# Seven block products for eight at two more sites of a four-layer graph network, and adjacency loads issued from another queue

## The chip, the core and the metric

The kernel runs on one NeuronCore of a Trainium2 chip. The metric is the device time of one execution in microseconds (us); lower is better. The engines are named as the profile names them: PE is TensorE (its matmuls; PEld is its weight loads), DVE is VectorE, ACT is ScalarE, POOL is GpSimd, SP is SyncE. ACTq and SPq are the queues of ScalarE and SyncE when they issue DMAs (transfers between the chip's main memory and its on-chip memory).

## What is computed

Thirty-two independent graphs ("batches" b = 0 to 31) of 512 nodes with 128 features pass through four layers. `x` holds the features and `adj` a dense 512 x 512 matrix for each graph. Everything is fp32. Each layer adds its result to its input:

```
h = relu(layernorm(x));  x = x + leaky_relu(normalised(adj + I) @ (h @ W) + b)             # layer 0
h = relu(layernorm(x));  x = x + tanh([adj @ in(h), node(h), adj^T @ out(h)] @ W_upd + b)   # layer 1
h = relu(layernorm(x));  x = x + f4                                                        # layer 2
h = relu(layernorm(x));  x = x + GRU(m, h), m = tanh(adj @ (h @ W_msg + b))                # layer 3
```

Layer 2 is itself a stack of four inner layers. With f0 = h, each computes f_new = tanh(A1 @ (f @ ws) + f @ wn + A2 @ (f @ wd) + b), where A1 and A2 are `adj` scaled to unit rows and to unit columns. The third inner layer takes [f2, f1] as its input and the fourth [f3, f1, f0], so their projections have 2 x 128 and 3 x 128 input features. The GRU of layer 3 has gates r and z, each a sum of a product of h and a product of m, and a third term whose two products stay apart.

## The kernel before, in words

**Planning.** The function `program(b)` (L389) doesn't issue instructions. It records operations with `op()`: an engine, an assumed duration, the buffers read and written, and a function that issues the instruction. For all 32 batches these go into one list. `Plan.order()` then plays the list through a model of the engines: each engine takes, from the operations whose inputs are ready and whose buffers have a free place, the one with the lowest key. The key is a due time (one batch every `PERIOD`, less the length of the work still behind the operation); the first batch's loads carry a `rank` that puts them ahead of everything. What comes out is one fixed order per engine. On the chip each engine works through its own order and never past an instruction that is still waiting. `places` says how many buffers of each kind exist ("bank": 8 PSUM banks of 512 fp32 per partition, "s2": 32 tiles of 128 x 512, "s4": 6 tiles of twice, "s8": 10 tiles of four times that size); `kept` says how many of a kind a younger batch has to leave free for each batch that is older and unfinished.

**A batch's work.** Loads of `x` (256 KB), `adj` as tile `a` and its transpose as tile `aT` (1 MB each, in two pieces of 512 KB; four of 256 KB for batch 0) go through `load()` at L405 and L413, all on SP. `adjt` is loaded a second time as `aT2` for layer 3, since layer 2 scales `a` and `aT` in place. `degree` (L608) and the squared norms (L687) are ACT passes over `a` and `aT`, called `sq`. A layernorm (L417 to L451) is DVE statistics, a power on POOL, and four ACT pieces `h` (L448). `aggregate` (L492) is four PE products of 512 columns into one PSUM bank. `turned` (L453) transposes through a DVE instruction and two DMA steps by way of main memory; in the first three and last two batches PE transposes instead (L484).

**Projections.** `paired_rows` (L510) makes both projections (ws and wd side by side, 256 columns wide) of the nodes, four chunks of 128 nodes each. For the third inner layer that is 4 chunks x 2 inputs = 8 products of 256 columns, with two DVE additions of bias (L523). The gates (L793 to L802) are, in all batches, 4 chunks of four products: two of 256 columns for r and z, and two of 128.

**`seven`** (L528) replaces a block product [x1 x2] @ [[b11, b12], [b21, b22]] of 2 x 2 blocks, each half of x being 256 nodes: seven block products stand in for eight, with sums of weights prepared once (`t_sb`, filled by `setup`, L375 to L387) and sums of inputs and of products made on DVE while it runs. A block product is two PE instructions of 128 columns (L567), so a use of `seven` has 14 of them, in four PSUM banks, and 14 DVE instructions: two of 512 columns (L580, L593) and twelve of 256 columns (L545). It needs five more s2 tiles. Before the change only the site "last" uses it: f1 and f0 of the fourth inner layer, as soon as f1 is known (L741). `program` already holds the code for the sites "mid" (L721) and "gates" (L781); both ask whether their name is in `SEVEN`.

Of the kernel before, what the change touches and what calls it, by code (L numbers as in the profile page):

```python
# [19 lines left out]
B, N, D = 32, 512, 128  # L20
NC = N // P
# [5 lines left out]
SMALL = 16  # L27


SEVEN = {"last": 0 * 5 * D}  # L30

T_COLS = 5 * D * len(SEVEN)

# [6 lines left out]
W_L2 = []  # L40
# [51 lines left out]
class Plan:  # L92
# [28 lines left out]
    def bank(self, name):  # L121
        return self.buf("bank", name=f"ps_{name}")

    def op(self, engine, us, emit, reads=(), writes=(), kb=0.0, rank=None, later=0.0):

        o = Op()
        o.engine, o.us, o.land, o.emit, o.batch, o.rank, o.later = engine, us, 0.0, emit, self.batch, rank, later
        if kb:  # L130
            o.us, o.land = max(us, kb / self.RATE), self.TRANSFER
        o.after, o.next, o.bufs = {}, [], []
        for group, written in ((reads, False), (writes, True)):
            for item in group:
                buf, part = item if isinstance(item, tuple) else (item, None)
                if written and buf.old is not None:
                    for other, _, _ in buf.old.uses:
                        o.after[other] = True
                for other, p, w in buf.uses:
                    if (w or written) and other is not o and (part is None or p is None or part & p):  # L140
                        o.after[other] = True
                buf.uses.append((o, part, written))
                if buf not in o.bufs:
                    o.bufs.append(buf)
        self.ops.append(o)
        return o
# [82 lines left out]
def gnn_stack(  # L229
# [11 lines left out]
    nc = tc.nc  # L241
    const = ctx.enter_context(tc.tile_pool(name="const", bufs=1))
    sb = ctx.enter_context(tc.tile_pool(name="sb", bufs=1))
    psum = ctx.enter_context(tc.tile_pool(name="psum", bufs=1, space=bass.MemoryType.PSUM))
    dram = ctx.enter_context(tc.tile_pool(name="dram", bufs=1, space=bass.MemoryType.DRAM))
    plan = Plan(sb, psum, {"bank": 8, "s2": 32, "s4": 6, "s8": 10}, {"bank": 1, "s2": 5, "s4": 0, "s8": 0})

    w_sb = const.tile([P, W_COLS], F32, name="w_sb")
    c_sb = const.tile([P, C_COLS], F32, name="c_sb")
# [1 line left out]
    rf_sb = const.tile([P, len(L2_CHUNKS) * 2 * D], F32, name="rf_sb")  # L251
# [15 lines left out]
    def t_tt(n, pointers=0):  # L267
        return 0.065 + 0.058 * pointers + n / 960
# [13 lines left out]
    def op(*args, **kwargs):  # L282
        return plan.op(*args, **kwargs)

    def const_buf(name, ap):
        b = Buf(plan, name, name, None)
        b.tile, b.slot = ap, 0
        return b

    W1, W2F, W3, CS, RS, RF, CF, TS, ID, NH = (const_buf(n, t) for n, t in (  # L290
        ("w1", w_sb), ("w2", w_sb), ("w3", w_sb), ("c_sb", c_sb), ("r_sb", r_sb), ("rf_sb", rf_sb),
        ("cf_sb", cf_sb), ("t_sb", t_sb), ("ident", ident), ("neg_half", neg_half)))

    def mm(ps, out_of, lhs, rhs, n, start, stop, reads, later=0.0):
        op("PE", t_mm(n), lambda: nc.tensor.matmul(out_of(ps.ap()), lhs(), rhs(), start=start, stop=stop),  # L295
           reads, [ps], later=later)

    def blocks(site):


        if site == "gates":
            return [c + k * D for c in (W_L3_HH, W_L3_IH) for k in range(2)], W3, (r_sb, R_L3_G), (RS, {2})
        i, k = {"mid": (2, 0), "last": (3, 1)}[site]
        at = W_L2[i][0] + k * 2 * D
        return [at + k * D for k in range(4)], W2F, (rf_sb, i * 2 * D), RF

    def setup():


        op("POOL", 1.0, lambda: make_identity(nc, ident), [], [ID])  # L310
        op("POOL", 0.2, lambda: nc.gpsimd.memset(neg_half, -0.5), [], [NH])
        first = W_L2[0][0]

# [29 lines left out]
        for i, (k, (proj, upd)) in enumerate(zip(L2_CHUNKS, RAW_L2, strict=True)):  # L343
# [23 lines left out]
            else:  # L367
# [5 lines left out]
                rf_sb[:, i * 2 * D:(i + 1) * 2 * D], ps.ap()[:, :2 * D]), [ps], [RF])  # L373
        for site, at in SEVEN.items():
            (b11, b12, b21, b22), wbuf, (bias, c), bbuf = blocks(site)  # L375
# [13 lines left out]
    def program(b):  # L389
        plan.batch = b  # L390

        def buf(tag, shape=(P, N), name=None):
            return plan.buf(tag, shape, name)
# [9 lines left out]
        pieces = NC if b == 0 else 2  # L403

        def load(dst, src, kb, rank):  # L405

            n = NC // pieces
            for k in range(pieces):
                s = slice(k * n, (k + 1) * n)
                op("SP", 0.4, lambda s=s: nc.sync.dma_start(dst.ap()[:, s, :], src[:, s, :]),  # L410
                   [], [(dst, set(range(NC)[s]))], kb=kb / pieces, rank=None if b else rank)

        op("SP", 0.4, lambda: nc.sync.dma_start(xt.ap(), x[b]), [], [xt], kb=256, rank=None if b else 0)  # L413
        load(a, adj[b], 1024, 1)
        load(aT, adjt[b], 1024, 4)

        def moments(xin, v8):  # L417
# [35 lines left out]
        def turned(m, name):  # L453


            blk, mT = buf("s2", rows_shape, "blk"), buf("s2", rows_shape, name)
            op("DVE", t_tt(N), lambda: nc.vector.transpose(
                blk.ap().rearrange("p b (c r) -> p c b r", c=NC), m.ap().rearrange(
                    "p c (b s) -> p c b s", b=NC) if len(m.shape) == 3 else m.ap().rearrange("p (c b s) -> p c b s", c=NC, b=NC)),
               [m], [blk])  # L460
            bounce = buf(f"turn_{name}", rows_shape)

            def away(k):
                if bounce.tile is None:
                    bounce.tile = dram.tile([P, NC, P], F32, name=bounce.name, tag=f"{bounce.kind}_{bounce.slot}", bufs=1)
                nc.sync.dma_start(bounce.tile[:, k, :].rearrange("(b s) n -> s b n", b=NC), blk.ap()[k * P // NC:(k + 1) * P // NC])

            for k in range(NC):
                op("SP", 0.4, lambda k=k: away(k), [blk], [(bounce, {k})], kb=64)
            op("SP", 0.4, lambda: nc.sync.dma_start(mT.ap(), bounce.tile), [bounce], [mT], kb=256)  # L470
            return mT

        def turned_cols(mT):
# [36 lines left out]
        def paired_rows(nodes, wcols, wbuf, bias, bbuf, col, sd=None):  # L510


            held, sd = sd, sd or buf("s4", (P, NC, 2 * D), "sd")
            for h in range(NC // 2):
                ps = plan.bank("sd")
                for j in range(2):
                    c = 2 * h + j
                    for k, nk in enumerate(nodes):
                        mm(ps, lambda t, j=j: t[:, j * 2 * D:(j + 1) * 2 * D],
                           lambda nk=nk, c=c: nk.ap()[:, c * P:(c + 1) * P],  # L520
                           lambda k=k: wt(wcols + k * 2 * D, 2 * D), 2 * D, k == 0, k == len(nodes) - 1, [nk, wbuf])
                part = (sd, set(range(4 * h, 4 * h + 4)))
                op("DVE", t_tt(N), lambda ps=ps, h=h: nc.vector.tensor_add(  # L523
                    sd.ap()[:, 2 * h:2 * h + 2, :], ps.ap().rearrange("p (j v) -> p j v", j=2),
                    sd.ap()[:, 2 * h:2 * h + 2, :] if held else along(bias, col, 2 * D, 2)), [ps, part if held else bbuf], [part])
            return sd

        def seven(site, x1, x2, dst, part):  # L528

            at = SEVEN[site]
            (b11, b12, b21, b22), wbuf, (bias, bc), bbuf = blocks(site)
# [124 lines left out]
        for h in range(2):  # L658
            s, part, halves = slice(2 * h, 2 * h + 2), {2 * h, 2 * h + 1}, set(range(4 * h, 4 * h + 4))
# [32 lines left out]
        bounce, spaced, rows = buf("bounce", (P, 2 * NC)), buf("s4", (P, P, 2 * NC), "spaced"), buf("s4", (P, 2, N), "rows")  # L692
# [24 lines left out]
        def of_halves(t):  # L717
            return (lambda k, o: t.ap()[:, 2 * k:2 * k + 2, o * D:(o + 1) * D]), (lambda k, o: (t, {4 * k + o, 4 * k + 2 + o}))

        for i, (wsd, wn) in enumerate(W_L2):  # L720
            if i == 2 and "mid" in SEVEN:  # L721
                sd = buf("s4", (P, NC, 2 * D), "sd")
                seven("mid", f[1], f[0], *of_halves(sd))
            elif i == 3 and "last" in SEVEN:
                sd = paired_rows(f[:1], wsd, W2F, rf_sb, RF, i * 2 * D, early)
# [4 lines left out]

            order = [(0, 0), (1, 1), (1, 0), (0, 1)] if i == 2 and "mid" in SEVEN else [(0, 0), (1, 0), (0, 1), (1, 1)]
            for h, o in order:
# [33 lines left out]
        psa = plan.bank("agg")  # L766
        aT2 = buf("s8", (P, NC, N), "aT2")
        load(aT2, adjt[b], 1024, None)
        aggregate(psa, msg, 0, aT2)
        mT = buf("s2", name="mT")  # L770
# [36 lines left out]
        for k in range(0, NC, w1):  # L807
            s, part, cols = slice(k, k + w1), set(range(k, k + w1)), 2 * D * w1
# [3 lines left out]
        for k in range(0, NC, w2):  # L812
            s, part, cols = slice(k, k + w2), set(range(k, k + w2)), w2 * D
# [66 lines left out]
```

## Time and profile before

| what | before |
|---|---|
| device time, median of 3 runs | 2338.86 us (2337.11 to 2338.99) |
| span of the profiled execution | 2338.4 us |
| PE busy | 2308.9 us, 8850 records |
| DVE busy | 1271.3 us, 3370 instructions |
| ACT busy | 947.3 us, 2018 instructions |
| POOL busy | 255.8 us |
| bytes moved by DMA | 196.45 MB, mean 84 GB/s |

A matmul in fp32 leaves two records in this profile, so 8850 PE records stand for half as many instructions. The matmuls are pipelined and the end of a record is modelled; how many one has room for in a given time is read from the distance between the starts of instructions that follow each other. The chain of work that ended last runs through PE for 93% of the span: what PE has to do, and where it sits idle, sets the time.

### The profile page before, as it was taken

How to read it: one execution, taken by the hardware profiler on the slowest of the kernel's cores; microseconds unless marked ns; L12 is line 12 of the kernel's file. 1: busy time of each engine (PE TensorE's matmuls, PEld its weight loads, DVE VectorE, ACT ScalarE, POOL GpSimd, SP SyncE). 2: the span in 40 equal slices, each digit the busy share in tenths (PEclk: the TensorE clock that was granted, in tenths of full speed). 3: DMA queues.
4: the chain of work that ended last, by engine and by line, in shares of the span. 5: the costliest groups of instructions: out<-in, count | busy, mean ns of one | idle time of the engine just before them, and what ended most of it. 6: DMA issues, size and time to landing. Idle time of an engine off the chain costs nothing.

```text
span 2338.4 us, 25489 instructions
## 1 busy us (share of the span) xinstructions
PE 2308.9 (99%) x8850; PEld 1431.8 (61%) x8850; DVE 1271.3 (54%) x3370; ACT 947.3 (41%) x2018; POOL 255.8 (11%) x218
## 2 busy tenths in 40 slices
PE   6999999999999999999999999999999999999998
PEld 5666566666666665666666666656666666656655
DVE  4446445655546655456555456555565554555634
ACT  7444144443434434434434344334444344433312
POOL 3111011101111101111011111011110101101001
PEclk9999999999999999999999999999999999999999
DMA  6122213223323233232333232332322332322000
GB/s 236 69 73 64 68 48 111 86 90 95 91 72 99 80 100 97 68 99 86 90 95 96 67 108 74 98 95 76 92 86 90 98 97 63 109 68 90 14 14 9
DMA packets 127280, 196.45 MB, mean 84 GB/s; under 512 B 18352, under 2 KB 75184, under 8 KB 127152
## 3 DMA queue, kind: packets, MB, share of 16 engines
q1 hardware_dynamic: 126864, 194.71, 27.3%
q8 instruction: 69, 1.13, 0.2%
q14 instruction: 59, 0.48, 0.1%
q10 hardware_dynamic: 288, 0.13, 0.0%
HBM read 157.95 MB, written 36.83 MB: 83 GB/s over the span
## 4 chain that ended last, share of the span: by engine, by line
PE 93%; DVE 3%; ACT 2%; DMA 1%; issue 0%; POOL 0%; SPq 0%; DVEq 0%; POOLq 0%; ACTq 0%
PE ps_agg L295 61%; PE ps_sd L295 14%; PE ps_gate L295 7%; PE ps_seven L567 4%; PE ps_upd L295 3%; PE ps_msg L295 1%; PE ps_lin L295 1%; PE ps_node L295 1%; ACT h L448 1%; DMA turn_f4r<-blk 0%; ACT rows L705 0%; DMA raw<-in_raw 0%; DMA f4r<-turn_f4r 0%; DVE bn L420 0%; DVE sd L523 0%
## 5 line engine op out<-in xcount | busy, mean ns | idle before, releaser
L295 PE MATMUL ps_agg<-aT,sd 128*128 128x512 f32 x1024 | 512.2, 593 | 0.2 <-DVE sd L523 0.2
L295 PE MATMUL ps_agg<-a,sd 128*128 128x512 f32 x1024 | 511.1, 593 | 0.0
L295 PE MATMUL ps_sd<-w_sb,f 128*128 128x256 f32 x1280 | 373.3, 381 | 1.4 <-ACT f L486 0.7
L436 POOL TENSOR_TENSOR sc<-v,neg_half 128x4 f32<-128x4 f32 (+1 forms) x128 | 150.7, 1178 | 1900.9 <-DVE v L423 1837.7
L295 PEld LDWEIGHTS ps_sd<-w_sb,f 128*128 128x128 f32 x1280 | 227.1, 191 | 138.7 <-issue 108.6
L295 PEld LDWEIGHTS ps_agg<-aT,sd 128*128 128x128 f32 x1024 | 180.9, 191 | 100.2 <-issue 89.9
L448 ACT ACTIVATE h<-xr,nb,sc 128x128 f32<-128x128 f32 x384 | 157.9, 482 | 178.2 <-DVE nb L444 176.8
L295 PE MATMUL ps_agg<-f,w_sb 128*128 128x512 f32 x448 | 229.7, 594 | 0.0
L295 PEld LDWEIGHTS ps_agg<-a,sd 128*128 128x128 f32 x1024 | 176.8, 191 | 83.2 <-issue 76.6
L523 DVE TENSOR_TENSOR sd<-ps_sd,rf_sb 128x512 f32<-128x512 f32 x192 | 130.8, 682 | 150.8 <-PE ps_sd L295 150.6
L738 ACT ACTIVATE f<-ps_agg,cf_sb 128x512 f32<-128x512 f32 x128 | 87.4, 683 | 210.6 <-PE ps_agg L295 210.6
L800 DVE TENSOR_TENSOR g<-ps_gate,r_sb 128x512 f32<-128x512 f32 x128 | 80.5, 684 | 148.6 <-PE ps_agg L295 135.4
L448 ACT ACTIVATE h<-x,nb,sc 128x128 f32<-128x128 f32 x128 | 53.1, 482 | 235.9 <-DVE nb L444 235.8
L295 PEld LDWEIGHTS ps_gate<-w_sb,mT 128*128 128x128 f32 x512 | 91.4, 190 | 73.2 <-issue 69.1
L295 PE MATMUL ps_agg<-aT,rep 128*128 128x512 f32 x256 | 130.7, 593 | 1.6 <-DVE rep L663 1.6
L295 PE MATMUL ps_agg<-a,rep 128*128 128x512 f32 x256 | 130.4, 592 | 0.0
L295 PE MATMUL ps_agg<-aT,msg 128*128 128x512 f32 x256 | 130.2, 593 | 0.0
L523 DVE TENSOR_TENSOR sd<-ps_sd,sd 128x512 f32<-128x512 f32 x64 | 44.2, 691 | 151.3 <-PE ps_sd L295 151.3
L705 ACT COPY rows<-spaced 128x1024 f32<-128x1024 f32 x32 | 65.8, 2055 | 149.0 <-DMA spaced<-bounce 147.5
L295 PE MATMUL ps_gate<-w_sb,mT 128*128 128x256 f32 (+1 forms) x512 | 118.6, 327 | 0.0
L295 PEld LDWEIGHTS ps_gate<-w_sb,hT 128*128 128x128 f32 x512 | 87.0, 191 | 48.5 <-issue 43.5
L295 PE MATMUL ps_gate<-w_sb,hT 128*128 128x128 f32 (+1 forms) x512 | 114.7, 327 | 0.0
(127 smaller groups left out, 3311.8 us busy)
## 6 DMA issues: line engine op xcount, KB each, us to landing
aT<-in_adjt SPq DMA_DIRECT2D x124, 512.0 KB, 4.8
a<-in_adj SPq DMA_DIRECT2D x62, 512.0 KB, 4.7
turn_turned<-blk SPq DMA_DIRECT2D x324, 64.0 KB, 1.8
turned<-turn_turned SPq DMA_DIRECT2D x81, 256.0 KB, 2.7
spaced<-bounce SPq DMA_DIRECT2D x32, 512.0 KB, 4.2
x<-in_x SPq DMA_DIRECT2D x32, 256.0 KB, 5.1
out<-xo SPq DMA_DIRECT2D x30, 256.0 KB, 2.3
turn_f4r<-blk SPq DMA_DIRECT2D x108, 64.0 KB, 3.6
```

The source lines that it names most:

```text
L295: op("PE", t_mm(n), lambda: nc.tensor.matmul(out_of(ps.ap()), lhs(), rhs(), start=start, stop=stop), reads, [ps], later=later)
L436: op("POOL", t_pow(n), lambda: nc.gpsimd.tensor_tensor(inv.ap()[:, :n], v8.ap()[:, :n], neg_half[:, :n], op=ALU.pow), [v8, NH], [(inv, {0})])
L448: op("ACT", t_act(D, 2), lambda c=c: nc.scalar.activation(h.ap()[:, c, :], xin.ap()[:, c, :], AF.Relu, bias=nb.ap()[:, c:c + 1], scale=inv ...
L523: op("DVE", t_tt(N), lambda ps=ps, h=h: nc.vector.tensor_add(sd.ap()[:, 2 * h:2 * h + 2, :], ps.ap().rearrange("p (j v) -> p j v", j=2), s ...
L567: op("PE", t_mm(D), lambda j=j: nc.tensor.matmul(ps.ap()[:, k * H + j * D:k * H + (j + 1) * D], lhs()[:, j * P:(j + 1) * P], rhs(), start= ...
L705: op("ACT", t_act(2 * N), lambda: nc.scalar.copy(rows.ap().rearrange("p s (c n) -> p (s c) n", c=NC), spaced.ap().rearrange("p n k -> p k ...
L738: op("ACT", t_act(N, 1), lambda ps=ps, i=i, f_new=f_new: nc.scalar.activation(f_new.ap(), ps.ap(), AF.Tanh, bias=cf_sb[:, i:i + 1]), [ps, ...
L800: op("DVE", t_tt(N), lambda ps=ps, c=c: nc.vector.tensor_add(g.ap()[:, c, :], ps.ap(), r_sb[:, R_L3_G:R_L3_G + 4 * D]), [ps, RS], [(g, fie ...
```

## The change

`SEVEN` gains the sites "mid" (the projections of [f2, f1] for the third inner layer, in all batches) and "gates" (the r and z gates, in all batches but the last two). The pairing of weight blocks and inputs is turned round for "mid" and adapted for "last". One PE product is saved in eight at each site; the sums that replace it are DVE work.

The loads of `a`, `aT` and `aT2` of the batches from the third on are issued by ScalarE's queue rather than SyncE's (the load of `x` itself stays on SP), so that they no longer stand in SP's order with the transposes' transfers. The planner is told longer landing times (`land`) for loads, and each younger batch has to leave one s8 tile free per older one.

```diff
-SEVEN = {"last": 0 * 5 * D}
+SEVEN = {"last": 0 * 5 * D, "mid": 1 * 5 * D, "gates": 2 * 5 * D}
...
-    def op(self, engine, us, emit, reads=(), writes=(), kb=0.0, rank=None, later=0.0):
+    def op(self, engine, us, emit, reads=(), writes=(), kb=0.0, rank=None, later=0.0, land=0.0):
...
-        o.engine, o.us, o.land, o.emit, o.batch, o.rank, o.later = engine, us, 0.0, emit, self.batch, rank, later
+        o.engine, o.us, o.land, o.emit, o.batch, o.rank, o.later = engine, us, land, emit, self.batch, rank, later
         if kb:
-            o.us, o.land = max(us, kb / self.RATE), self.TRANSFER
+            o.us, o.land = max(us, kb / self.RATE), self.TRANSFER + land
...
-    plan = Plan(sb, psum, {"bank": 8, "s2": 32, "s4": 6, "s8": 10}, {"bank": 1, "s2": 5, "s4": 0, "s8": 0})
+    plan = Plan(sb, psum, {"bank": 8, "s2": 32, "s4": 6, "s8": 10}, {"bank": 1, "s2": 5, "s4": 0, "s8": 1})
...
-        i, k = {"mid": (2, 0), "last": (3, 1)}[site]
-        at = W_L2[i][0] + k * 2 * D
-        return [at + k * D for k in range(4)], W2F, (rf_sb, i * 2 * D), RF
+        i, order = {"mid": (2, (1, 0)), "last": (3, (1, 2))}[site]
+        return [W_L2[i][0] + (2 * k + o) * D for k in order for o in range(2)], W2F, (rf_sb, i * 2 * D), RF
...
-                op("SP", 0.4, lambda s=s: nc.sync.dma_start(dst.ap()[:, s, :], src[:, s, :]),
-                   [], [(dst, set(range(NC)[s]))], kb=kb / pieces, rank=None if b else rank)
+                if b < 2:
+                    op("SP", 0.4, lambda s=s: nc.sync.dma_start(dst.ap()[:, s, :], src[:, s, :]),
+                       [], [(dst, set(range(NC)[s]))], kb=kb / pieces, rank=None if b else rank, land=1.0)
+                else:
+
+                    op("ACT", 0.45, lambda s=s: nc.scalar.dma_start(dst.ap()[:, s, :], src[:, s, :]),
+                       [], [(dst, set(range(NC)[s]))], land=kb / pieces / plan.RATE + 3.0)
...
-            op("SP", 0.4, lambda: nc.sync.dma_start(mT.ap(), bounce.tile), [bounce], [mT], kb=256)
+            op("SP", 0.4, lambda: nc.sync.dma_start(mT.ap(), bounce.tile), [bounce], [mT], kb=256, land=0.5)
```

## The prediction

> **What bounds the kernel now.** I read the page's busy shares and slices first, then the steady stretches, then the start.
>
> ```profile
> PE 2308.9 (99%) x8850; PEld 1431.8 (61%) x8850; DVE 1271.3 (54%) x3370; ACT 947.3 (41%) x2018; POOL 255.8 (11%) x218
> PE   6999999999999999999999999999999999999998
> PEclk9999999999999999999999999999999999999999
> ...
> PE 93%; DVE 3%; ACT 2%; DMA 1%; issue 0%; POOL 0%; SPq 0%; DVEq 0%; POOLq 0%; ACTq 0%
> ```
>
> PE is full in every slice but the first and last, at full clock; the chain of waits agrees. Four stretches as long as one batch's period (71.32 us, the distance at which a run of twelve aggregation records comes back in the chain), with PE, PEld, DVE, ACT and POOL busy in that order:
>
> ```profile
> 571.32:642.64 71.32, 71.32 (x274) 44.17 (x273) 39.78 (x106) 29.52 (x63) 7.55 (x6) 1.00 0.30 88
> 642.64:713.96 71.32, 71.32 (x274) 44.17 (x273) 40.04 (x106) 29.42 (x63) 7.55 (x6) 1.00 0.30 90
> ```
>
> There is no hole in PE here, so an instruction less on PE is time less. Of the 29.5 us in which PE idles, two thirds lie at the start:
>
> ```profile
> 0.00:14.10 14.10, 3.12 (x14) 3.12 (x15) 2.06 (x12) 6.27 (x16) 4.10 (x12) 1.00 0.88 288
> 14.10:33.30 19.20, 14.80 (x96) 12.52 (x94) 7.76 (x32) 14.74 (x40) 4.43 (x4) 1.00 0.72 261
> 33.30:60.00 26.70, 22.93 (x89) 14.54 (x90) 20.00 (x76) 25.25 (x68) 10.64 (x8) 0.87 0.54 193
> ```
>
> 11.0, 4.4 and 3.8 us of idle, and the DMA engines 88% busy in the first stretch: the start waits for data. When batch 0's first `h` can be made stands in ACT's timeline:
>
> ```profile
> 9.17 0.63 ACT L608 ACTIVATE sq<-a 128x512 f32<-128x512 f32 x1
> 9.71 0.19 ACT L608 ACTIVATION_READ_ACCUMULATOR sq<-a 128x1 f32 x1
> 12.51 1.65 ACT L448 ACTIVATE h<-x,nb,sc 128x128 f32<-128x128 f32 x4 [2.61 <-DVE nb L444]
> ```
>
> Every product of layer 0 waits for that `h` at 12.51 us.
>
> [...] The trace agrees that busy time misleads (one record lasts longer than the distance to the next), so I price PE by the distance between starts. [...] The trace of before can't show sharing (ScalarE issues two small DMAs in it), but it shows the engines at 1.0 of their time from 4 to 20 us. I conclude that batch 2's loads on ACT's queue slow batch 0's. [...]
>
> **PE.** Pace first, from starts that follow each other:
>
> ```profile
> 1343.36 1.89 PE L295 MATMUL ps_sd<-w_sb,hT 128*128 128x256 f32 x8
> 1345.09 1.02 PE L295 MATMUL ps_agg<-a,sd 128*128 128x512 f32 x2
> 1382.23 1.05 PE L295 MATMUL ps_msg<-w_sb,hT 128*128 128x128 f32 x8
> 1383.12 1.02 PE L295 MATMUL ps_agg<-a,sd 128*128 128x512 f32 x2
> ```
>
> Eight records are four products: 1.73 us / 4 = 0.4325 us at 256 columns, 0.89 / 4 = 0.2225 at 128. "mid" removes 8 products of 256 columns (3.460 us) and adds 14 of 128 (3.115): 0.345 us less, which is less than an eighth because the narrow ones pay a fixed part. The r and z gates are the same: 8 go, 14 come, 0.345. With 32 uses of "mid" and 30 of "gates" that is 62 x 0.345 = **21.4 us off PE**; the built program agrees (868 more products of 128 columns, 496 fewer of 256). The period would fall from 71.32 to 70.63 us.
>
> **DVE.** The 14 instructions of one `seven` add up, over the rows of "last", to 201.3 us for 32 uses, 6.29 us each. "mid" saves two bias additions (L523, 0.682 each), "gates" two of its four (L800, 0.684): +4.93 and +4.92 us a batch. DVE goes from 40.0 to 49.8 us of 70.63, 71%: not the bound, and priced at nothing as throughput because it lies beside PE. Ten weight sums more in setup, 0.29 us each, lie in DVE's idle time of the start.
>
> **Latency, the unknown.** Each new `seven` puts DVE sums between a product and its reader, and takes four PSUM banks. What hides that is other batches' PE work, so I looked at how much of it the new order leaves. Nearest case: the tanh that makes f2. Before, five pieces of another batch's layer 0 follow (128, 384, three more; some 1.75 us); now five 128-column products, 1.11 us. The chain itself takes 0.20 us from the last product to ACT (product ends 1342.50 at the pace, tanh starts 1342.70), 0.69 for the tanh, 0.05 back to PE (hT copy ends 28.86, product at 28.91): 0.94. That leaves 0.17 us where 0.8 was left. Four or five places a batch are like it: a copy of agg_in, tanh f3, two bias additions into `sd`, the chain into `rep`. In each PE loses time only if ACT or DVE is late by over 0.1 to 0.3 us, and DVE is full for some 5 us around two of them. Lower bound 0, upper bound 0.5 us a batch (three of five late by 0.17): 0 to 15 us. I take 0.1 a batch, **+3 us**.
>
> **Loads on ACT's queue.** Six a batch from batch 2, 180 in all; an issue there takes 0.41 and 0.46 us in the trace, so 2.6 us a batch on ACT, which idles 42 of 71 us: nothing, as throughput. Each may wait for its buffer or for a landing, and behind it wait all of ACT's passes. In the steady part the awaited DMA is one issued 8 to 25 us earlier, against 2 to 5 us to landing: nothing. SP's queue is freed of waits, but no PE time waited for it: no gain.
>
> **The start, where I expect the loss.** The loads of batches 2 and 3 have nothing to wait for, so they stand first in ACT's order:
>
> ```
> aT_2, w, aT_2, r, a_2, a_2 | sq_2, aT_3, sq_2, aT_3, sq_2, 5 of sq_0 and sq_2, a_3, sq_0, sq_3, a_3, sq_3, w copy, sq_3, sq_0, h_0
> ```
>
> Before, ACT ran four passes over batch 0 and then `h_0`. Now the first pass is one over `a_2`, and `h_0` sits behind the second half of `a_3`. Step by step: by the windows DMA moved 238 GB/s in the first 10 us and 405 in the next 10. Ahead of `a_2`'s first half lie about 3 MB of both queues: it lands near 11 to 13 us. Seven passes at 0.76 us (start to start, 9.17 less 8.42 in the timeline) and two issues bring ACT to 18 to 20 us. Then `a_3` half by half, each to landing in 4.7 us,
>
> ```profile
> a<-in_adj SPq DMA_DIRECT2D x62, 512.0 KB, 4.7
> ```
>
> (the second is issued after a pass over the first): 9.4 + 0.8 + two passes 1.5 gives 29.5 to 32 us for `h_0`, 17 to 19.5 later. PE has only folds of weights meanwhile. Some comes back: batches 1 to 3 are on chip earlier, and two whole layer 0 sums stand in the order where PE idled 3.8 us up to 60 us and 0.5 later; `aT_0` no longer trickles in (1 to 2 us of the 4.4). 17 less 5 is **+12 us**; bounds +6 (landing early, all idle refilled) and +20 (nothing refilled).
>
> **Sum.** 2338.9 - 21.4 + 12 + 3 = 2332.5 us.
>
> **Rivals.** (1) The start costs little: +6, latency 0: 2323.5; DMA's 405 GB/s after 10 us and batches 1 to 3 being on chip early speak for it, ACT's order against it. (2) Start and saving cancel: +18 to +20 and 2 to 3 of latency, 2338 to 2340; that PE has little else to do while it waits for `h_0` speaks for it; the 3.8 us of holes before 60 us, which new work can fill, against it. (3) Latency binds, slower than before: 0.4 to 0.5 us at each batch, 13 us, with +15 at the start gives 2345.5. For it: the slack of 0.17 us and the bursts of DVE. Against it: every planned gap is positive, and the plan's prices (0.60 us between starts of two 512-column DVE instructions) match the trace.
>
> **Chances.** My case 0.40, (1) 0.19, (2) 0.19, (3) 0.22. The bound of 0.2% is 4.7 us, at 2334.2 and 2343.5. Faster: all of (1) and most of mine, 0.36: 0.55. Same: (2) and the rest of mine, 0.23. Slower: 0.22. For 8 in 10 the range goes from 2319, a little under (1), to 2348, just over (3).
>
> **What would show it.** Right: period 70.6 us, `h_0` at about 30 us in ACT's timeline, PE idle of some 27 us up to 33 us, PE still without holes in the middle. Wrong: `h_0` before 20 us (then the start was mispriced); PE idle before `f` or `sd` readers in the middle (then latency was); a period that didn't fall by 0.69 us (then the pace).

## The result, and the profile after

| | before | after |
|---|---|---|
| device time, median | 2338.93 us (2337.11 to 2339.02, 4 runs) | 2449.93 us (2449.05 to 2454.39, 4 runs) |
| ratio | | 1.048, 95% interval 1.0462 to 1.0499 |
| span of the profiled execution | 2338.4 us | 2447.2 us |
| PE busy | 2308.9 us | 2331.5 us |
| DVE busy | 1271.3 us | 1510.6 us |

The kernel is 111 us slower, where 6 us faster was forecast. The page of after, with the rows that answer to those shown of before:

```profile
PE 2331.5 (95%) x9594; PEld 1451.2 (59%) x9594; DVE 1510.6 (62%) x4124; ACT 925.6 (38%) x2018; POOL 256.4 (10%) x218
...
PE   4999999999999999999999999999999999999898
...
PEclk8999999999999999999999999999999999999999
```

A 9 in the slices means 90% or more, so the loss doesn't show in them: PE went from 99% to 95% of a longer span. The chain of waits can't be compared, since in this trace it could be followed back over the last stretch only (its shares add up to some 5% of the span). What shows the loss is windows. Two stretches of one old period, the same as shown of before, where PE was busy for all of the 71.32 us; then the start (columns: window and its length; busy time of PE, PEld, DVE, ACT and POOL; granted clock; DMA share; GB/s):

```profile
571.32:642.64 71.32, 69.54 (x296) 43.47 (x295) 48.17 (x133) 25.44 (x52) 7.57 (x6) 1.00 0.26 79
642.64:713.96 71.32, 68.12 (x273) 41.73 (x272) 44.31 (x122) 28.74 (x62) 7.63 (x6) 0.98 0.30 91
...
0.00:14.10 14.10, 0.00 (x0) 0.00 (x0) 1.32 (x9) 1.28 (x1) 2.00 (x8) 1.00 0.86 279
14.10:33.30 19.20, 5.21 (x24) 5.12 (x24) 1.22 (x6) 7.76 (x23) 4.53 (x6) 0.75 1.03 405
33.30:60.00 26.70, 19.32 (x86) 14.44 (x87) 10.28 (x43) 20.76 (x59) 5.24 (x4) 0.73 0.36 107
```

PE has holes in the steady part, and its clock is not always full. The batches come every 74.55 us (third and 24th issue of f4r's copy, 523.29 and 2088.81 us, 21 batches apart), where they came every 71.32.

**A balance.** To keep slow clock and idle time apart I count PE's *work*: records of each width times their distance between starts in full stretches (0.1112 us at 128 columns, 0.2165 at 256, 0.4295 at 512; 0.3235 at 384, taken midway). Before has 2298.8 us of work, after 2277.1: the sevens took 22 us off PE. The 108.8 us between the spans are then:

| term | from | us |
|---|---|---|
| work | 2277.1 - 2298.8 | -21.7 |
| PE idle, first 100 us | 36.7 - 19.7 | +17.0 |
| PE idle, 100 to 2100 us | 59.3 - 1.0 | +58.3 |
| PE idle, from 2100 us to the end | 19.7 - 8.8 | +10.9 |
| PE busy beyond its work | (2331.5 - 2277.1) - (2308.9 - 2298.8) | +44.3 |

Of the last term the clock accounts for about 24 us: by the traces' records of the clock, 53.9 us of PE's busy time in after ran at half clock, 5.5 us in before, and half of the difference is lost (below, 3.30 us for what takes 1.72 at full clock). Some 20 us I can't assign.

**One hole.** The timeline of after around 1270 us, cut to the instructions that matter (start, length, engine, line, tiles; in brackets the idle time before and who ended it):

```profile
1258.96 0.93 ACTq L414 DMA_DIRECT2D aT<-in_adjt  x2
1259.92 1.12 ACTq L414 DMA_DIRECT2D aT<-in_adjt  x2
...
1261.31 2.30 SPq L470 DMA_DIRECT2D turn_f4r<-blk  x4
...
1269.39 0.34 SPq L474 DMA_DIRECT2D f4r<-turn_f4r  x1
...
1272.20 0.69 DVE L758 TENSOR_TENSOR xr<-xr,f4r 128x512 f32<-128x512 f32 x1 [5.46 <-DMA f4r<-turn_f4r]
...
1274.37 0.42 DVE L549 TENSOR_TENSOR s<-f,s 128x256 f32<-128x256 f32 x1
...
1274.84 1.38 PE L571 MATMUL ps_seven<-t_sb,s 128*128 128x128 f32 x8 [3.20 <-DVE s L549]
...
1276.85 3.47 PE L295 MATMUL ps_agg<-aT,sd 128*128 128x512 f32 x4 [0.41 <-DVE sd L549]
```

Four loads of 512 KB leave within the 2.4 us ahead of f4r's transpose, whose second step starts 8.1 us after the first piece was issued. DVE reaches `xr`, which needs f4r, and stands there for 5.46 us. Behind it in DVE's order are the sums that a `seven` is waiting for, and DVE doesn't pass over `xr` to them (all 4124 DVE instructions of this trace start in the order of the program), so PE stands too. PE comes back at 1274.84 us, and about 1.6 us later its clock falls: four records of 512 columns then take 3.30 us from start to start of what follows (1276.85 to 1280.15 us), against 1.72 at the usual distance:

```profile
1276.00:1277.00 1.00, 0.59 (x5) 0.40 (x4) 1.00 (x5) 0.84 (x3) 0.00 (x0) 0.73 0.00 0
1277.00:1278.00 1.00, 1.00 (x2) 0.48 (x3) 0.88 (x3) 1.00 (x4) 0.00 (x0) 0.50 0.00 0
1278.00:1279.00 1.00, 1.00 (x3) 0.48 (x2) 1.00 (x3) 0.31 (x1) 0.00 (x0) 0.50 0.00 0
1279.00:1280.00 1.00, 1.00 (x2) 0.39 (x2) 0.19 (x1) 0.00 (x0) 0.00 (x0) 0.56 0.36 87
1280.00:1281.00 1.00, 1.00 (x5) 0.76 (x4) 0.00 (x0) 0.00 (x0) 0.00 (x0) 1.00 0.56 135
```

These are some 3.4 us at 0.50 (by the shares of the first and last window), after a hole of 3.2 us. From 500 to 2200 us PE has twelve holes of 2.7 to 4.4 us, and each goes with 3.4 or 6.8 us at half clock, which begin between 1.4 us before and 2.2 us after its end. (Two more holes, of 2.6 us at 377 us and of 3.0 us at 2305, go with none.) The twelve are 41.6 us of idle time, and 43.4 us of busy time at half clock, of which half is lost, go with them: such a hole is paid about one and a half times.

**Every second batch.** These holes come two batches apart, as do the slower ones of two kinds of f4r's transposes. Of the 27 transposes thirteen, every second one, have four loads issued between 4 us before and 3 us after their first piece, and their copy is issued 7.5 to 9.1 us after that piece. The other fourteen have two such loads, and their copy is issued after 4.9 to 6.7 us. A hole of 2.6 to 4.4 us follows each of the thirteen, and of the fourteen only the last.

Over the run, from the waits (total us, times, longest):

```profile
DVE xr L758 <- DMA f4r<-turn_f4r: 95.1, 27, 6.6
...
PE ps_seven L571 <- DVE s L549: 45.1, 15, 4.3
```

Before, xr waited 7.4 us in all and PE never for a sum of a `seven`.

### The profile page after: what moved, and what is told of

The parts are those of the page before. It is cut to its first block, busy times and chain, and to the rows that moved or that the text cites. A ratio compares the mean times of both kernels' runs of the same rounds, so it can differ in the third digit from the quotient of the medians.

```text
span 2447.2 us, 28102 instructions
## 1 busy us (share of the span) xinstructions
PE 2331.5 (95%) x9594; PEld 1451.2 (59%) x9594; DVE 1510.6 (62%) x4124; ACT 925.6 (38%) x2018; POOL 256.4 (10%) x218
## 5 line engine op out<-in xcount | busy, mean ns | idle before, releaser
L571 PEld LDWEIGHTS ps_seven<-t_sb,s 128*128 128x128 f32 x1128 | 167.1, 196 | 123.3 <-issue 58.7
L571 PE MATMUL ps_seven<-t_sb,s 128*128 128x128 f32 x1128 | 182.8, 283 | 45.1 <-DVE s L549 45.1
L295 PE MATMUL ps_sd<-w_sb,f 128*128 128x256 f32 x768 | 222.0, 381 | 1.5 <-ACT f L493 0.7
L295 PEld LDWEIGHTS ps_sd<-w_sb,f 128*128 128x128 f32 x768 | 137.8, 190 | 122.7 <-issue 89.0
L527 DVE TENSOR_TENSOR sd<-ps_sd,rf_sb 128x512 f32<-128x512 f32 x128 | 87.6, 685 | 92.4 <-PE ps_sd L295 90.5
L612 ACT ACTIVATE sq<-a 128x512 f32<-128x512 f32 x128 | 79.2, 619 | 105.3 <-DMA a<-in_adj 105.0
L571 PEld LDWEIGHTS ps_seven<-w_sb,f 128*128 128x128 f32 x512 | 79.7, 191 | 49.4 <-issue 44.2
L527 DVE TENSOR_TENSOR sd<-ps_sd,r_sb 128x512 f32<-128x512 f32 x64 | 44.0, 689 | 93.1 <-PE ps_sd L295 93.1
L295 PE MATMUL ps_agg<-aT,h 128*128 128x256 f32 (+2 forms) x384 | 101.1, 386 | 0.0
L597 DVE TENSOR_TENSOR ev<-ps_seven,ev 128x512 f32<-128x512 f32 x94 | 64.1, 681 | 59.4 <-PE ps_seven L571 59.0
```

The source lines that it names most:

```text
L527: op("DVE", t_tt(N), lambda ps=ps, h=h: nc.vector.tensor_add(sd.ap()[:, 2 * h:2 * h + 2, :], ps.ap().rearrange("p (j v) -> p j v", j=2), s ...
L571: op("PE", t_mm(D), lambda j=j: nc.tensor.matmul(ps.ap()[:, k * H + j * D:k * H + (j + 1) * D], lhs()[:, j * P:(j + 1) * P], rhs(), start= ...
L597: op("DVE", t_tt(N), lambda: nc.vector.tensor_add(ev.ap(), bank_b.ap()[:, None, :H].to_broadcast([P, 2, H]), ev.ap()), [bank_b, ev], [ev])
L612: op("ACT", 0.73, lambda c=c: nc.scalar.activation(sq.ap(), a.ap()[:, c, :], AF.Copy, accum_out=stat.ap()[:, c:c + 1]), [(a, {c})], [sq, ( ...
```

## The experiments

A *promise* is the time by which the plan takes a transfer to have landed; the *middle* is the stretch from 100 to 2100 us. Theory 1 when they began: the moved loads collide with the transposes' transfers, because they now come through a second queue. Theory 2: the sevens are too tight and the loads have no part. All kernels here compute the whole result; line numbers in the counting kernels are 3 higher than in after. The ratio is to the kernel before, on the same chip.

### Each half of the change without the other

All loads on SP, sevens at all three sites:

```diff
-                if b < 2:
+                if b < B:
```

> The kernel after with every load of x and adjacencies on SP's queue; seven products at all three sites. Theory 1 (the loads on ScalarE's ring collide with the transposes' transfers, the waits for f4r and turned block VectorE and ScalarE in order): batches at about 70.6 us, h_0 near 13 us, no wait of xr for f4r above 1 us; 2315 to 2325 us. Theory 2 (the sevens are too tight for VectorE, the loads have no part in it): batches stay near 74.9 us and only the start's 16 us come back; 2430 to 2436 us.

Measured: 2330.9 us, ratio 0.997 (0.9957 to 0.9982). Loads on ScalarE's queue, but the sevens of before only:

```diff
-SEVEN = {"last": 0 * 5 * D, "mid": 1 * 5 * D, "gates": 2 * 5 * D}
+SEVEN = {"last": 0 * 5 * D}
```

> Seven products at the last third projection alone, as before, with the loads on ScalarE's queue as after. Theory 1: the collision is there without the new sevens; xr waits for f4r by 3 to 6 us in most batches, and the run is 2410 to 2470 us. Theory 2: only the start is dearer, some 16 us, so 2350 to 2358 us.

Measured: 2588.75 us, ratio 1.1071 (1.1049 to 1.1093), slower than either theory said, and not through the wait that theory 1 named: xr waits 34.2 us for f4r, PE 128.2 us in 40 for the bias sums `sd` of L527. Theory 2 is out: without the moved loads the sevens are slightly faster than before, and without the new sevens the moved loads do still more harm. With all loads on SP the middle is full:

```profile
100.00:1100.00 1000.00, 999.06 (x4177) 624.75 (x4176) 658.59 (x1782) 389.10 (x825) 115.54 (x81) 1.00 0.26 79
1100.00:2100.00 1000.00, 998.38 (x4180) 625.42 (x4179) 672.74 (x1817) 408.74 (x877) 124.13 (x84) 1.00 0.30 91
```

### Two repairs that missed

Batches 2 and 3 on SP as well:

```diff
-                if b < 2:
+                if b < 4:
```

> The kernel after with the loads of batches 0 to 3 on SP's queue instead of batches 0 and 1. If the late start comes from the loads of batches 2 and 3 that stand ahead of ScalarE's first products: h_0 at 13 to 14 us and 14 to 18 us less than after, 2432 to 2436 us, batches unchanged at 74.9 us. If it comes from the adjacency loads on SP themselves: h_0 stays near 35 us and the time within 3 us of after.

Measured: 2469.47 us, ratio 1.0561 (1.054 to 1.0582). `h_0` starts at 26.65 us, not 13: ScalarE still issues six loads, now of batches 4 and 5, and runs 14 passes over adjacencies before it. The first 100 us win 4 us of PE time, and the rest of the run, through the same waits, loses more than that (xr for f4r: 97.9 us in 27). Longer promises for the transposes:

```diff
-                op("SP", 0.4, lambda k=k: away(k), [blk], [(bounce, {k})], kb=64)
+                op("SP", 0.4, lambda k=k: away(k), [blk], [(bounce, {k})], kb=64, land=2.0)
-            op("SP", 0.4, lambda: nc.sync.dma_start(mT.ap(), bounce.tile), [bounce], [mT], kb=256, land=0.5)
+            op("SP", 0.4, lambda: nc.sync.dma_start(mT.ap(), bounce.tile), [bounce], [mT], kb=256, land=4.0)
```

> The kernel after with the transposes' transfers planned to land later (2.0 us more for each piece, 3.5 us more for the copy back). Theory 1: the plan puts the readers of f4r and turned later, VectorE no longer stands in order behind them; xr's wait falls from 95 us to below 30 us, the batches go to 70.6 to 72.5 us and the time to 2345 to 2395 us. Theory 2: no effect beyond 1%, 2425 to 2470 us.

Measured: 2525.29 us, ratio 1.08 (1.0778 to 1.0821). xr's wait does disappear, and the order gets worse: now PE waits for what the later transposes feed, `ps_sd` for `f` 50.8 us in 11 waits of up to 19.9. My reading, which no run tests: a later promise for every transpose is a longer chain for every batch, and the buffers don't hold enough other work to fill it.

### The queue, or the plan?

The move did two things: the load is *issued* by another queue, and it is *planned* as 0.45 us of ScalarE in place of 2.13 us of SP's modelled queue (512 KB at RATE). These can be had one without the other. Planned on SP, issued by ScalarE:

```diff
-                if b < 2:
-                    op("SP", 0.4, lambda s=s: nc.sync.dma_start(dst.ap()[:, s, :], src[:, s, :]),
+                if True:
+                    op("SP", 0.4, lambda s=s: (nc.sync if b < 2 else nc.scalar).dma_start(dst.ap()[:, s, :], src[:, s, :]),
```

> The order of work that the planner makes with all loads on SP (as in the all-SP run), but the loads of batches 2 to 31 are then issued by ScalarE's queue at the same planned place. If the second ring by itself does the harm (loads and transposes share the engines, ScalarE stands behind the loads' waits), the time is near after: 2400 to 2460 us. If the harm is in the plan, which takes the loads to cost no transfer time and packs them, the time stays near the all-SP run: 2325 to 2350 us.

Planned as in after, issued by SP:

```diff
-                    op("ACT", 0.45, lambda s=s: nc.scalar.dma_start(dst.ap()[:, s, :], src[:, s, :]),
+                    op("ACT", 0.45, lambda s=s: nc.sync.dma_start(dst.ap()[:, s, :], src[:, s, :]),
```

> The order of work that the planner makes for after (loads taken to cost ScalarE 0.45 us and nothing of the transfers), but every load issued by SP's queue. If the second ring does the harm: 2325 to 2360 us. If the plan does: 2400 us or more, with xr and f still waiting for f4r and turned, since the transposes then stand in line behind the packed loads.

| planned as | issued by SP | issued by ScalarE |
|---|---|---|
| SP, 2.13 us a load | 2330.9 us (ratio 0.997) | 2330.96 us (ratio 0.9964, 0.9949 to 0.9979) |
| ScalarE, 0.45 us | 2475.93 us (ratio 1.0588, 1.0567 to 1.0609) | 2449.93 us (ratio 1.048) |

Theory 1 falls as far as the queue goes: the second queue costs nothing here (0.06 us in the upper row), and with the plan of after it is even 26 us the faster. The queues' rows of the first run (packets, MB, share of 16 engines) show that it did carry the loads:

```profile
q1 hardware_dynamic: 100944, 100.32, 14.8%
q10 hardware_dynamic: 26208, 94.51, 12.1%
```

With the plan of after on SP alone the waits are as in after:

```profile
DVE xr L758 <- DMA f4r<-turn_f4r: 90.8, 27, 5.6
...
PE ps_seven L571 <- DVE s L549: 41.6, 25, 3.4
```

So theory 3: the harm is in the order. The planner takes the moved loads' transfers for free, and promises what is transferred beside them too early. How long a piece of f4r's transpose took from issue to landing (the last number, a median) fits; in after, then with all loads on SP:

```profile
turn_f4r<-blk SPq DMA_DIRECT2D x108, 64.0 KB, 5.5
...
turn_f4r<-blk SPq DMA_DIRECT2D x108, 64.0 KB, 1.8
```

### Counting the transfers

If that is it, one fact given back to the planner of after must restore the middle, the loads staying on ScalarE:

```diff
                 event(now + o.us, "idle")
+                if e == "ACT" and o.land:
+                    idle_at["SP"] = max(idle_at["SP"], now) + o.land - 3.0
+                    event(idle_at["SP"], "idle")
```

> The kernel after, but the planner keeps SP's modelled queue busy for the transfer of every load that ScalarE issues (2.13 us for 512 KB). Theory 3 (the harm is that the plan takes the moved loads' transfers for free and so promises the transposes too early): xr's wait for f4r falls from 95 us to below 25 us and no middle stretch of PE is under 98% busy; the start stays late, as ScalarE's loads now also hold back SP's first ones; 2345 to 2368 us. Theory 4 (ScalarE is disturbed by issuing and waiting for the loads): no better than after, 2440 us or more.

Measured: 2379.06 us, ratio 1.0173 (1.0151 to 1.0195), 71 us faster than after. xr waits 7.6 us in all, and PE idles 7.1 us in the middle. It missed its range at the start: PE waits 42.1 us for `h_0`, since the first loads of batches 2 and 3 now hold SP's modelled queue as well. The same, from 20 us of the plan on (`and now > 20.0` added to the condition):

> As the run in which the planner counts the moved loads' transfers against SP, but only from 20 us of the plan on, so that the start is that of after. Theory 3: start as in after (h_0 near 36 us, some 17 us more TensorE idle than before), a dense middle: 2343 to 2356 us. If the loads on ScalarE disturb the middle by themselves: above 2400 us.

Measured: 2357.97 us (2351.89 to 2361.42), ratio 1.0078 (1.0045 to 1.0111), two us above its range. Its start is that of after (PE busy 64.75 us of the first 100; after 63.34), its middle is full:

```profile
100.00:1100.00 1000.00, 995.37 (x4127) 618.51 (x4126) 653.20 (x1759) 377.90 (x803) 104.90 (x77) 1.00 0.26 79
1100.00:2100.00 1000.00, 998.52 (x4190) 625.88 (x4189) 669.33 (x1821) 404.12 (x870) 115.71 (x84) 1.00 0.30 89
```

xr waits 4.9 us in 4 waits, after 95.1 in 27. In after these 2000 us held 59.3 us of idle PE; here 6.1. Both sides changed, the promise and the transfers. From the first piece's issue to the issue of f4r's copy, planned (the planner's own start times) and measured, medians:

| kernel | planned | measured |
|---|---|---|
| all loads on SP | 2.95 us | 3.25 us |
| after | 2.95 us | 6.66 us |
| after, counted from 20 us on | 5.22 us | 6.25 us |

With all loads on SP the promise is as early as in after, and it is kept: 26 of the 27 transposes have no load issued between 4 us before and 3 us after their first piece. The counted kernel comes closer from both ends. Twelve of its transposes have no such load and the others two, so that the longest takes 7.6 us in place of 9.1; and the plan puts xr 8.45 us after the first piece (measured 9.77), where that of after put it at 5.87 (measured 9.44).

### The move alone, in the kernel before

The edit to `load` and nothing else:

```diff
+                if b < 2:
                     op("SP", 0.4, lambda s=s: nc.sync.dma_start(dst.ap()[:, s, :], src[:, s, :]),
                        [], [(dst, set(range(NC)[s]))], kb=kb / pieces, rank=None if b else rank)
+                else:
+                    op("ACT", 0.45, lambda s=s: nc.scalar.dma_start(dst.ap()[:, s, :], src[:, s, :]),
+                       [], [(dst, set(range(NC)[s]))], land=kb / pieces / plan.RATE + 3.0)
```

> The kernel before with one part of the change alone: the loads of batches 2 to 31 are planned and issued on ScalarE's queue, no added landing times, no place kept, sevens at one site. Theory 3 (transfers taken for free): slower than before by the start's 17 us and by a thinned middle, 2390 us or more. If the harm needs the sevens or the other edits: 2350 to 2358 us, the start alone.

Measured: 2398.32 us, ratio 1.0261 (1.0208 to 1.0314). And with the counting from 20 us on:

> The same, but from 20 us of the plan on every load that ScalarE issues also keeps SP's modelled queue busy for its transfer. Theory 3: the middle is dense again and only the start is lost, 2350 to 2368 us. Otherwise no better than the run without the counting.

Measured: 2351.6 us, ratio 1.0061 (1.0038 to 1.0083). PE in the two halves of the middle is busy 985.17 and 982.33 us in the first, 998.34 and 1000.00 in the second; what remains is the start (66.94 us busy of the first 100, before 80.33). The two ACT waits for a turned block fall most, 236.9 to 46.8 us for `hT` and 99.4 to 31.7 for `f`. xr still waits, 38.8 us in 26, and is still later than planned (9.37 us after the first piece, planned 5.37), but no PE wait follows. So here a late transfer cost nothing by itself, only through what stood behind its reader. What PE lost in the first run stood behind ACT's waits:

```profile
PE ps_sd L295 <- ACT f L742: 37.9, 27, 5.3
```

In the second this wait is 2.2 us in 2. But f4r's promise isn't what the counting mended here: it stayed as early (2.95 us to the copy in both plans, measured 6.63 and then 6.80), and nearly every transpose has two loads beside it in both. That the transfers must be counted is shown in both kernels; that the uncounted ones do their harm through f4r's promise is shown in after only. Which change of the order helped here stays open.

### The landing times and the kept place

On SP's queue with the sevens at three sites, only the added landing times vary:

| loads `land` | copy back `land` | time | ratio |
|---|---|---|---|
| 0 | 0 | 2387.89 us | 1.0213 (1.0196 to 1.0231) |
| 0 | 0.5 | 2352.63 us | 1.006 (1.0038 to 1.0081) |
| 1.0 | 0.5 | 2330.9 us | 0.997 (0.9957 to 0.9982) |
| 1.0 | 1.0 | 2366.32 us | 1.0116 (1.0098 to 1.0134) |

> All loads on SP's queue and the sevens at all three sites, without the added landing times (1.0 us for a load, 0.5 us for the transpose's copy back), so as before but for the sevens. If the landing times matter little beside the sevens: 2326 to 2336 us. If they carry the all-SP run's gain: 2338 us or more.

> All loads on SP, sevens at three sites, 0.5 us added to the landing of the transposes' copy back, nothing to the loads'. If the transposes' promise is what decides: within 6 us of the all-SP run, 2327 to 2338 us. If the loads' 1.0 us decides: near the run without both, 2375 to 2392 us.

> All loads on SP, sevens at three sites, 1.0 us in place of 0.5 us added to the transposes' copy back and 1.0 us to the loads. If what is left of the stalls comes from transposes that still land later than planned: 2322 to 2329 us. If the longer promise only shifts the order: 2329 to 2345 us.

The first came out as the second of its cases; the other two missed both of theirs. Half a microsecond in the copy back's promise moves the time by 35 us, in either direction, and a whole one in the loads' by 22. PE's work is the same in all four (2277.1 us), the holes are not. Without the landing times the waits that reach PE are small and many (total us, times, longest):

```profile
PE ps_agg L295 <- DVE sd L549: 18.1, 37, 1.5
...
PE ps_sd L295 <- ACT hT L493: 10.6, 25, 0.9
```

Why 1.0 us at the copy back is worse than 0.5 stays open.

An order as touchy as this is also a rival for the counting: no run holds SP's modelled queue for as long at other places, so how much of that gain is a luckier order isn't shown. Luck alone it hardly is. The six kernels planned without the moved loads' transfers are 2.6 to 10.7% slower than before, the three that count them 0.6 to 1.7%.

Last, the two new sites undone, with all loads on SP and the landing times, with a large buffer kept and without (`"s8": 1`, `"s8": 0`):

> The all-SP run with the two new sites of seven products undone (only the last third projection has them, as before); landing times and the kept place stay. If the sevens are worth the 22 us of dense TensorE time that the records show and the rest is equal: 2345 to 2356 us. If the other edits (landing times, the place kept) fit the plan with one site badly: above 2360 us, with idle TensorE time in the middle.

> The one-site kernel with all loads on SP and the added landing times, but with no place of the large buffers kept. If the kept place made the one-site run slow (2384 us): 2335 to 2350 us. If the landing times did: 2375 us or more.

Measured: 2384.45 us, ratio 1.0197 (1.0167 to 1.0226), and 2347.71 us, ratio 1.0042 (1.0022 to 1.0062). With one site the kept place costs 37 us, and so part of the 2588.75 us above is probably its doing. With three sites the plan comes to no end without it. The second is the fairest one-site kernel to set against 2330.9 us: 17 us for the two sites, near the 22 us of their work.

The version with all loads on SP beats both kernels; planned on SP and issued by ScalarE it is as fast.

## Why the prediction was wrong, point by point

**PE, -21.4 us: right.** The records give 21.7. With all loads on SP the kernel even came out at 2330.9 us, but not for the reasons of the forecast of 2332.5: no late start, and 12 us more time without work than before (2329.1 - 2277.1 = 52.0 against 39.6).

**DVE at nothing as throughput: right.** At 1519.7 us busy, DVE left the middle of the all-SP run full.

**The start, +12 us: right in the order it read, a little small.** `h_0` starts at 35.82 us in ACT's timeline, behind both halves of `a_3`, as the order said:

```profile
27.71 0.63 ACT L612 ACTIVATE sq<-a 128x512 f32<-128x512 f32 x1 [5.96 <-DMA a<-in_adj]
...
34.58 0.63 ACT L612 ACTIVATE sq<-a 128x512 f32<-128x512 f32 x1 [5.03 <-DMA a<-in_adj]
...
35.82 1.63 ACT L452 ACTIVATE h<-x,nb,sc 128x128 f32<-128x128 f32 x4
```

29.5 to 32 was forecast; the two halves took longer, ACT waiting 5.96 and 5.03 us for them. PE idles 17 us more in the first 100, inside the bounds of 6 and 20. What the forecast took as given is that the order is made from a wrong price. The planner's `lag()` asks for no landing where issuer and reader are the same engine, so it takes a piece of `a` that ScalarE loads to be readable 0.58 us after the issue (0.45 + 0.13). It plans the first pass over `a_2` at 1.8 us and `h_0` at 13.5; on the chip they start at 14.24 and 35.82. No run corrects this. In the middle it isn't the harm: counted from 20 us on, ACT still waits 125.6 us for `a` in 32 waits, and PE idles 6.1 us.

**"Loads on ACT's queue ... nothing", "SP's queue is freed of waits ... no gain": the step that failed.** It priced the move as work on two queues: 2.6 us a batch of issue on an engine that idles, and waits for loads long under way. ACT does wait for `a` (`sq`: 105.0 us in 32, before 3.5), but it does so for 97.2 us in 35 in the run planned on SP and issued by ScalarE, which lost nothing. What it left out is that the order of every engine is computed, and that this edit changed an input of the computation. `op("SP", ..., kb=512)` held the modelled queue for 2.13 us; `op("ACT", 0.45, ...)` holds nothing that a transpose needs. 180 loads x 2.13 us = 384 us of modelled transfer went out of the plan, while the chip still moved the same 94 MB. The lines were in the diff and the model in the code. The forecast looked at what the moved loads wait for, not at what is transferred beside them. Its own sentence on the start, that batch 2's loads slow batch 0's, was an inference that the trace of before could not show. After shows it: batch 0's four pieces of `a`, issued from 1.18 us on in both kernels, landed after 6.9 us in the median, before after 5.3. In the steady part, too, f4r's pieces were slow beside the moved loads (5.5 us in the median, 1.8 with all loads on SP); the sentence was not carried there. Shown by: the same order on either queue gives the same time to about 1% (2475.93, 2449.93) or better (2330.9, 2330.96), the move alone slows the kernel before by 2.6%, and the counting restores the middle in both.

**Latency, +3 us (0 to 15): the right place; the size fits the sevens alone.** With all loads on SP, PE idles 2.6 us in the middle, where it idled 1.0 before (33.2 without the landing times). In after PE does lose its time at DVE sums in front of a `seven`, `sd` and a turned block. It is 69 us of idle after the first 100 us, and 44 of slow clock and unassigned time on top. The slack was measured inside DVE and ACT; the delay came from a transfer, and DVE, which stood for it up to 6.6 us at `xr`, handed it on to all that followed in its order. A price for the half clock that went with the holes was not in the sum.

**Rivals.** The third, "latency binds", named the right side, at 2345.5 us. None had an order that fails as a whole.

## What to carry to other kernels

Where a planner writes the order, a change of queue is a change of the planner's prices: ask what the operation held in the model before, what holds it now, and who was being kept away by it. Move the issue and leave the cost where it was: that was free here, and with the cost gone from the plan the kernel took 119 us more (2449.93 against 2330.96). And when an order leaves PE no slack, treat a promise for a transfer as a constant to be tuned by measuring: here half a us more in it gained 35 us at one place and cost 35 at another.

## What the runs showed of the hardware

- A second issuing queue changed the time by nothing that can be told: 2330.9 us with all loads on SP and 2330.96 us planned on SP and issued by ScalarE, with 94.5 MB on the one queue or the other. The pieces of f4r's transpose landed a little later (2.8 us against 1.8 in the median), within what the order could bear.
- A hole of 3.2 us in PE was followed by some 3.4 us at half clock, which made four records of 512 columns take 3.30 us in place of 1.72. Two of the twelve holes that went with half clock were 2.74 us long. Over the run, the mean clock was 0.985, before 0.998, and in the one-site kernel with moved loads 0.97; there PE was busy for 2388.9 us with 2298.8 us of work.
